# The last two steps of a graph network: products three blocks behind the sums, 62 row buffers, bias and residual from PSUM

## The chip, the core and the metric

The kernel runs on one core of one Trainium2 chip. A core has TensorE (PE in the profile), VectorE (DVE), ScalarE (ACT), GpSimd (POOL) and SyncE (SP), which run side by side and wait for each other through semaphores, and 16 DMA engines that move data between the chip's memory (DRAM) and the on-chip memories SBUF and PSUM. SBUF has 128 partitions. PSUM, where TensorE writes, has eight banks of 128 x 512 float32. The metric is the device time of one launch in microseconds (us); lower is better.

## The reference

Two layers over a graph of N = 10000 nodes and E = 160000 edges, with rows of 512 float32 numbers. The first layer (a relational layer with layer norms and a small MLP) isn't touched here. The second is two SAGE steps:

```python
def _sage_layer(h, src, dst, W_self, W_neigh, b, n_nodes):
    agg = jax.ops.segment_sum(h[src], dst, num_segments=n_nodes)
    deg = jax.ops.segment_sum(jnp.ones_like(dst, dtype=h.dtype), dst, num_segments=n_nodes)
    h_neigh = agg / jnp.maximum(deg, 1.0)[:, None]
    return jax.nn.relu(h @ W_self + h_neigh @ W_neigh + b)

h = jnp.maximum(_layernorm(x, axis=-1), 0.0)
x = x + _L1_gnn_ref(h, src, dst, ...)     # two calls of _sage_layer, one after the other
```

Each step gathers one row of `h` per edge, sums the rows by target node, divides by the degree, multiplies node and mean by a 512 x 512 matrix each, and adds a bias. The second step's output is added to `x`.

## The kernel before, in words

Three parts run one after the other. The first makes the per-relation products of all nodes and, beside them, sorts the edges into lists: for each block of 128 nodes, twelve lists of one edge per node (`row1` for the SAGE steps) and a list of at most 720 more edges for the nodes with a higher degree (`ovr1`), as six tiles of up to 128 rows. The second part is the first layer's sums with its MLP. The third part, two SAGE steps from line 764 on, is what the change touches. There are 79 blocks: the last one has 16 nodes and is taken first.

One block of a SAGE step goes like this. `gather` (line 493) issues 18 indirect DMAs on POOL, six for the longer list and then twelve with one row per node, each into a buffer of a ring of 32 (`RING`). `hots` (L505, VectorE) makes a 0/1 matrix that sends the 720 rows to their nodes; `sums` (L516, TensorE) multiplies it with the six tiles and leaves the sum in a PSUM bank `pa`, of which there are two. `add` (L527, VectorE) adds the twelve other tiles to it in place. ScalarE scales it by 1/degree into `m` (L822). `transposed` (L159 on TensorE, L160 on ScalarE) turns `m` into `mT`, and likewise the block's own rows `hb`, loaded by `load` (L780), into `hT` (`turn`). Four matmuls with `wss` (L825) and four with `wns` (L795) go to one bank `po`. `finish` adds the bias (L798, VectorE) and then, in the first step, applies ReLU on ScalarE (L804) and stores to `h2_d` (L805), or, in the second, takes the maximum with 0 and adds the residual `res` (L800, loaded at L784), and stores to `out` (L802). Float32 matmuls show in the profile as two records each.

The order is written out by hand: each engine runs its instructions in the order in which the program names them, and waits on semaphores where a value isn't there. The tile framework sets these waits, also for a buffer that is to be used again. In iteration i of a step the order is: load block i+2; mask of i+1; adds of i; scaling of i; the products of i with `wss`; `finish` of i-1, which holds its products with `wns`; `turn` of i+1; gathers and sums of i+1; transposes of `m` of i. All loads and stores of a step go through SP's queue, all gathers through POOL's. A step can gather only when the step before has stored all its rows.

Of the kernel before, what the change touches and what calls it, by code (L numbers as in the profile page):

```python
# [21 lines left out]
def kernel(  # L22
# [455 lines left out]
    def aligned(ctxa):  # L478

        gat = ctxa.enter_context(tc.tile_pool(name="gat", bufs=1))  # L480
        psA = ctxa.enter_context(tc.tile_pool(name="psA", bufs=2, space=PSUM))
        RING = 32
# [3 lines left out]
        def height(b):  # L486
            return min(P, N - b * P)

        def gather(b, table, row, ovr):

            def rows(n, idx):
                t = gat.tile([P, D], F32, name="rows", bufs=RING)
                nc.gpsimd.indirect_dma_start(  # L493
                    out=t[:n], out_offset=None, in_=table,
                    in_offset=bass.IndirectOffsetOnAxis(ap=idx, axis=0))
                return t[:n]

            others = [rows(n, ovr[:n, b, t:t + 1]) for t, n in enumerate(ov_tiles(b))]
            r = height(b)
            return others, [rows(r, row[:r, b, t:t + 1]) for t in range(T)]  # L500
# [29 lines left out]
        with ExitStack() as s:  # L530
            wp = s.enter_context(tc.tile_pool(name="wp2", bufs=1))
# [231 lines left out]

        for step, (h_d, ws, wn, bs) in enumerate(((h1_d, ws1, wn1, bs1), (h2_d, ws2, wn2, bs2))):
            with ExitStack() as s:
                wp = s.enter_context(tc.tile_pool(name="wp3", bufs=1))
                ip = s.enter_context(tc.tile_pool(name="ip", bufs=2))
                psT = s.enter_context(tc.tile_pool(name="psT3", bufs=3, space=PSUM))
                psO = s.enter_context(tc.tile_pool(name="psO3", bufs=3, space=PSUM))
# [5 lines left out]
                loaded, hTs = {}, {}  # L775

                def load(b):
                    r = height(b)
                    h = ip.tile([P, D], F32, name="hb", bufs=4)
                    nc.sync.dma_start(h[:r], h_d[b * P:b * P + r, :])  # L780
                    res = None
                    if step:
                        res = ip.tile([P, D], F32, name="res", bufs=5)
                        nc.sync.dma_start(res[:r], xn_d[b * P:b * P + r, :])  # L784
                    loaded[b] = (h, res)

                def turn(b):
                    r = height(b)
                    hTs[b] = ip.tile([P, KC, P], F32, name="hTb")
                    transposed(psT, hTs[b][:, :, :r], loaded[b][0][:r], r)  # L790

                def finish(b, po, mT):
                    r = height(b)
                    for k in range(KC):
                        nc.tensor.matmul(po[:r], mT[:, k, :r], wns[:, k, :], start=False,  # L795
                                         stop=(k == KC - 1))
                    o = ip.tile([P, D], F32, name="ob", bufs=3)
                    nc.vector.tensor_tensor(o[:r], po[:r], bss[:r], op=OP.add)  # L798
                    if step:
                        nc.vector.scalar_tensor_tensor(o[:r], o[:r], 0.0, loaded[b][1][:r],  # L800
                                                       op0=OP.max, op1=OP.add)
                        nc.sync.dma_start(out[b * P:b * P + r, :], o[:r])  # L802
                    else:
                        nc.scalar.activation(o[:r], o[:r], AF.Relu)  # L804
                        nc.sync.dma_start(h2_d[b * P:b * P + r, :], o[:r])  # L805
                    del loaded[b]

                for b in blocks[:2]:
                    load(b)
                turn(blocks[0])  # L810
                before = None
                held = begin(blocks[0], hots(blocks[0]), h_d, row1, ovr1)
                for i, b in enumerate(blocks):
                    r = height(b)
                    if i + 2 < len(blocks):
                        load(blocks[i + 2])
                    if i + 1 < len(blocks):
                        hot = hots(blocks[i + 1])
                    pa, own = held
                    add(b, pa, own)  # L820
                    m = ip.tile([P, D], F32, name="mb")
                    nc.scalar.activation(m[:r], pa[:r], AF.Copy, scale=rdeg[:r, b:b + 1])  # L822
                    po = psO.tile([P, D], F32, name="po3")
                    for k in range(KC):
                        nc.tensor.matmul(po[:r], hTs[b][:, k, :r], wss[:, k, :], start=(k == 0),  # L825
                                         stop=False)
                    if before:
                        finish(*before)
                    if i + 1 < len(blocks):
                        turn(blocks[i + 1])  # L830
                        held = begin(blocks[i + 1], hot, h_d, row1, ovr1)
                    mT = ip.tile([P, KC, P], F32, name="mTb")
                    transposed(psT, mT[:, :, :r], m[:r], r)
                    before = (b, po, mT)
                finish(*before)
# [308 lines left out]
```

## Time and profile before

| | us |
|---|---|
| median of 3 runs | 7879.0 (7872.07 to 7888.42) |
| profiled execution | 7907.2 |
| its span, first to last instruction | 7905.4 |
| first gather of the first layer's sums, in the span | 1591.5 |
| first gather of the first SAGE step | 3786.7 |
| first gather of the second SAGE step | 5844.8 |

The profile is of one execution. PE, DVE, ACT and POOL stand for the engines; PEld are TensorE's weight loads. A row of the groups gives line, engine, operation, output and inputs, the number of instructions, then their busy time and the mean in ns, then the idle time of the engine ahead of them and what ended most of it ("remote" is another core or an unknown queue, "issue" is time in which the profile shows nothing that was waited for). In the order of time a line has its start, its length, the engine, and in brackets how long the engine stood idle before it. Matmuls' ends are modelled in this profile. Over the whole span PE was busy 70%, DVE 47%, POOL 53%, ACT 13%; the DMA engines moved 182 GB/s.

### The profile page before, as it was taken

How to read it: one execution, taken by the hardware profiler on the slowest of the kernel's cores; microseconds unless marked ns; L12 is line 12 of the kernel's file. 1: busy time of each engine (PE TensorE's matmuls, PEld its weight loads, DVE VectorE, ACT ScalarE, POOL GpSimd, SP SyncE). 2: the span in 40 equal slices, each digit the busy share in tenths (PEclk: the TensorE clock that was granted, in tenths of full speed). 3: DMA queues.
4: the chain of work that ended last, by engine and by line, in shares of the span. 5: the costliest groups of instructions: out<-in, count | busy, mean ns of one | idle time of the engine just before them, and what ended most of it. 6: DMA issues, size and time to landing. Idle time of an engine off the chain costs nothing.

```text
span 7905.4 us, 50392 instructions
## 1 busy us (share of the span) xinstructions
PE 5555.9 (70%) x13686; PEld 2485.8 (31%) x13686; DVE 3693.7 (47%) x6357; ACT 1016.7 (13%) x1667; POOL 4174.9 (53%) x4346
## 2 busy tenths in 40 slices
PE   6969999947888888888555555665555665555565
PEld 3434444413333333334222222222222222222222
DVE  5424666345666666665243333344334444334434
ACT  0000000012222222223100000000000000000000
POOL 0030000066666666663566666666656666666665
PEclk9989999968888888889777787777777777777777
DMA  3232222266777777774566666666656666676765
GB/s 141 96 103 96 101 101 93 82 194 199 221 217 211 216 213 216 215 217 143 176 201 198 197 204 201 201 200 198 198 173 210 210 210 207 208 215 211 211 211 173
DMA packets 492503, 1441.17 MB, mean 182 GB/s; under 512 B 85650, under 2 KB 85650, under 8 KB 482082
## 3 DMA queue, kind: packets, MB, share of 16 engines
q0 software_dynamic: 337136, 1088.57, 47.1%
q1 hardware_dynamic: 141170, 262.13, 9.5%
q10 hardware_dynamic: 13904, 87.17, 2.8%
q8 instruction: 111, 1.82, 0.1%
q14 instruction: 182, 1.49, 0.1%
HBM read 1230.52 MB, written 207.01 MB: 182 GB/s over the span
## 4 chain that ended last, share of the span: by engine, by line
PE 41%; issue 26%; another core or an unknown queue 22%; DVE 4%; ACT 3%; DMA 2%; POOL 2%; ACTq 0%; POOLq 0%; DVEq 0%
PE pm L459 17%; PE pa L516 7%; PE ph L598 6%; PE po L608 5%; PE po L795 3%; PE po L825 3%; DVE pa L527 2%; POOL rows L493 2%; ACT hTb L160 1%; PE pT L159 1%; DMA n_i<-in_dst_dram 0%; ACT mTb L160 0%; DMA rows<-h_d,ovr 0%; DMA rows<-hall_d,row 0%
## 5 line engine op out<-in xcount | busy, mean ns | idle before, releaser
L527 DVE TENSOR_TENSOR pa<-pa,rows 128x512 f32<-128x512 f32 (+1 forms) x2844 | 1987.0, 699 | 1575.3 <-issue 1134.2
L493 POOL DMA_INDIRECT rows<-h_d,row x1896 | 1822.3, 961 | 1004.1 <-issue 498.4
L795 PE MATMUL po<-wns,mTb 128*128 128x512 f32 (+1 forms) x1264 | 753.2, 751 | 1260.6 <-issue 722.3
L516 PE MATMUL pa<-rows,hot 128*128 128x512 f32 (+2 forms) x2814 | 1331.5, 618 | 181.6 <-issue 141.9
L493 POOL DMA_INDIRECT rows<-hall_d,row x948 | 938.0, 989 | 506.2 <-issue 224.5
L493 POOL DMA_INDIRECT rows<-h_d,ovr x938 | 889.7, 948 | 488.1 <-issue 213.1
L459 PE MATMUL pm<-wrel,hT 128*128 128x512 f32 (+1 forms) x2528 | 1100.2, 593 | 18.2 <-issue 18.2
L493 POOL DMA_INDIRECT rows<-hall_d,ovr x469 | 445.1, 949 | 1222.0 <-issue 1146.8
L825 PE MATMUL po<-wss,hTb 128*128 128x512 f32 (+1 forms) x1264 | 716.0, 719 | 424.4 <-ACT hTb L160 322.9
L795 PEld LDWEIGHTS po<-wns,mTb 128*128 128x128 f32 (+1 forms) x1264 | 298.7, 244 | 1700.8 <-issue 1132.7
L516 PEld LDWEIGHTS pa<-rows,hot 128*128 128x128 f32 (+2 forms) x2814 | 539.8, 197 | 853.5 <-issue 800.1
L598 PE MATMUL ph<-x1T,w1s 128*128 128x512 f32 (+2 forms) x1344 | 616.0, 612 | 205.8 <-issue 143.0
L798 DVE TENSOR_TENSOR ob<-po,bss 128x512 f32<-128x512 f32 (+1 forms) x158 | 108.7, 688 | 1288.3 <-remote 978.3
L459 PEld LDWEIGHTS pm<-wrel,hT 128*128 128x128 f32 (+1 forms) x2528 | 478.0, 189 | 627.4 <-issue 609.0
L608 PE MATMUL po<-w2s,hid 128*128 128x512 f32 (+1 forms) x1264 | 592.5, 615 | 84.6 <-issue 74.1
L825 PEld LDWEIGHTS po<-wss,hTb 128*128 128x128 f32 (+1 forms) x1264 | 278.4, 232 | 759.8 <-issue 420.6
L462 DVE TENSOR_TENSOR ha<-pm,brel 128x512 f32<-128x512 f32 (+1 forms) x316 | 217.8, 690 | 582.5 <-PE pm L459 539.0
L598 PEld LDWEIGHTS ph<-x1T,w1s 128*128 128x128 f32 x1344 | 267.1, 207 | 525.0 <-issue 444.3
L608 PEld LDWEIGHTS po<-w2s,hid 128*128 128x128 f32 (+1 forms) x1264 | 242.1, 195 | 393.4 <-issue 374.0
L459 PE MATMUL pm<-wself,hT 128*128 128x512 f32 (+1 forms) x632 | 296.3, 611 | 55.9 <-issue 33.7
L160 ACT COPY mTb<-pT 128x512 f32<-128x512 f32 (+1 forms) x158 | 92.1, 583 | 1716.2 <-remote 1472.6
L340 POOL IOTA tags<- 128x79 f32 x1 | 0.3, 282 | 446.3 <-DVE first_i L329 446.3
(174 smaller groups left out, 3297.7 us busy)
## 6 DMA issues: line engine op xcount, KB each, us to landing
hall_d<-ha ACTq DMA_DIRECT2D x78, 1024.0 KB
hb<-h_d SPq DMA_DIRECT2D x156, 256.0 KB
rows<-h_d,row POOLq DMA_INDIRECT x1896
xs<-xs_d SPq DMA_DIRECT2D x78, 256.0 KB
xr<-xr_d SPq DMA_DIRECT2D x78, 256.0 KB
xn_d<-xr SPq DMA_DIRECT2D x78, 256.0 KB
h_d<-h SPq DMA_DIRECT2D x78, 256.0 KB
h_d<-ob SPq DMA_DIRECT2D x78, 256.0 KB
```

Of the source, the lines that this page charges most:

```text
L159: nc.tensor.transpose(p[:, k, :r], rows[:, k * P:(k + 1) * P], ident[:r, :r])
L160: nc.scalar.copy(dest, p[:, :, :r])
L459: nc.tensor.matmul(pm[:r], hT[:, k, :r], w[:, k, :], start=(k == 0), stop=(k == KC - 1))
L462: nc.vector.tensor_tensor(ha[:r, j - 1, :], pm[:r], brel[:r, (j - 1) * D:j * D], op=OP.add)
L493: nc.gpsimd.indirect_dma_start(out=t[:n], out_offset=None, in_=table, in_offset=bass.IndirectOffsetOnAxis(ap=idx, axis=0))
L516: nc.tensor.matmul(pa[:r], hot[:k, t, :r], o, start=(t == 0), stop=(t == n - 1))
L527: nc.vector.tensor_tensor(pa[:r], pa[:r], t, op=OP.add)
L598: nc.tensor.matmul(ph[:, :n], w1s[:, k, f * P:(f + 1) * P], self.xT[:, k, :n], start=(k == 0), stop=(k == KC - 1))
L608: nc.tensor.matmul(po[:r], self.hid[:, f, c * r:(c + 1) * r], w2s[:, f, :], start=(f == 0), stop=(f == FC - 1))
L795: nc.tensor.matmul(po[:r], mT[:, k, :r], wns[:, k, :], start=False, stop=(k == KC - 1))
L798: nc.vector.tensor_tensor(o[:r], po[:r], bss[:r], op=OP.add)
L825: nc.tensor.matmul(po[:r], hTs[b][:, k, :r], wss[:, k, :], start=(k == 0), stop=False)
```

## The change

The two SAGE steps get their own ring of 62 row buffers and three banks for `pa` (the first layer keeps 32 and two); both are now opened in each step by `buffers`. The products with `wss` and `wns` move into one function, `products`, which runs three blocks behind the sums (`LAG = 3`); `hT`, `mT` of up to four blocks are kept. The order of iteration i becomes: load `hb` of i+2; load `res` of i-2; mask of i+1; products of i-3; `turn` of i; gathers and sums of i+1; adds and scaling of i; `finish` of i-3; transposes of `m` of i. Three more iterations close the step. `po` has two banks in place of three, `hb` three buffers in place of four, `res` three in place of five. In the second step the bias is added in place in PSUM, and the residual add reads that bank in place of `ob`.

```diff
@@ aligned
-        gat = ctxa.enter_context(tc.tile_pool(name="gat", bufs=1))
-        psA = ctxa.enter_context(tc.tile_pool(name="psA", bufs=2, space=PSUM))
-        RING = 32
+        gat, psA, ring = None, None, 0
...
+        def buffers(s, n, blocks):
+
+            nonlocal gat, psA, ring
+            gat = s.enter_context(tc.tile_pool(name="gat", bufs=1))
+            psA = s.enter_context(tc.tile_pool(name="psA", bufs=blocks, space=PSUM))
+            ring = n
+
...
-                t = gat.tile([P, D], F32, name="rows", bufs=RING)
+                t = gat.tile([P, D], F32, name="rows", bufs=ring)
...
         with ExitStack() as s:
+            buffers(s, 32, 2)
             wp = s.enter_context(tc.tile_pool(name="wp2", bufs=1))
...
+        LAG = 3
         for step, (h_d, ws, wn, bs) in enumerate(((h1_d, ws1, wn1, bs1), (h2_d, ws2, wn2, bs2))):
             with ExitStack() as s:
+                buffers(s, 62, 3)
                 wp = s.enter_context(tc.tile_pool(name="wp3", bufs=1))
-                ip = s.enter_context(tc.tile_pool(name="ip", bufs=2))
+                ip = s.enter_context(tc.tile_pool(name="ip", bufs=4))
                 psT = s.enter_context(tc.tile_pool(name="psT3", bufs=3, space=PSUM))
-                psO = s.enter_context(tc.tile_pool(name="psO3", bufs=3, space=PSUM))
+                psO = s.enter_context(tc.tile_pool(name="psO3", bufs=2, space=PSUM))
...
                 def load(b):
                     r = height(b)
-                    h = ip.tile([P, D], F32, name="hb", bufs=4)
...
+                    hbs[b] = ip.tile([P, D], F32, name="hb", bufs=3)
+                    nc.sync.dma_start(hbs[b][:r], h_d[b * P:b * P + r, :])
+
+                def load_res(b):
+                    r = height(b)
+                    ress[b] = ip.tile([P, D], F32, name="res", bufs=3)
+                    nc.sync.dma_start(ress[b][:r], xn_d[b * P:b * P + r, :])
...
-                def finish(b, po, mT):
+                    transposed(psT, hTs[b][:, :, :r], hbs.pop(b)[:r], r)
+
+                def products(b):
                     r = height(b)
-                    for k in range(KC):
-                        nc.tensor.matmul(po[:r], mT[:, k, :r], wns[:, k, :], start=False,
-                                         stop=(k == KC - 1))
+                    hT, mT = hTs.pop(b), mTs.pop(b)
+                    po = psO.tile([P, D], F32, name="po3")
+                    for t, w, first in ((hT, wss, True), (mT, wns, False)):
+                        for k in range(KC):
+                            nc.tensor.matmul(po[:r], t[:, k, :r], w[:, k, :],
+                                             start=(first and k == 0),
+                                             stop=(not first and k == KC - 1))
+                    return po
+
+                def finish(b, po):
+                    r = height(b)
                     o = ip.tile([P, D], F32, name="ob", bufs=3)
-                    nc.vector.tensor_tensor(o[:r], po[:r], bss[:r], op=OP.add)
                     if step:
-                        nc.vector.scalar_tensor_tensor(o[:r], o[:r], 0.0, loaded[b][1][:r],
+                        nc.vector.tensor_tensor(po[:r], po[:r], bss[:r], op=OP.add)
+                        nc.vector.scalar_tensor_tensor(o[:r], po[:r], 0.0, ress.pop(b)[:r],
                                                        op0=OP.max, op1=OP.add)
                         nc.sync.dma_start(out[b * P:b * P + r, :], o[:r])
                     else:
+                        nc.vector.tensor_tensor(o[:r], po[:r], bss[:r], op=OP.add)
                         nc.scalar.activation(o[:r], o[:r], AF.Relu)
                         nc.sync.dma_start(h2_d[b * P:b * P + r, :], o[:r])
...
+                n = len(blocks)
                 for b in blocks[:2]:
                     load(b)
-                turn(blocks[0])
-                before = None
                 held = begin(blocks[0], hots(blocks[0]), h_d, row1, ovr1)
-                for i, b in enumerate(blocks):
-                    r = height(b)
-                    if i + 2 < len(blocks):
+                for i in range(n + LAG):
+                    b = blocks[i] if i < n else None
+                    old = blocks[i - LAG] if i >= LAG else None
+                    if i + 2 < n:
                         load(blocks[i + 2])
-                    if i + 1 < len(blocks):
+                    if step and 0 <= i - LAG + 1 < n:
+                        load_res(blocks[i - LAG + 1])
+                    if i + 1 < n:
                         hot = hots(blocks[i + 1])
-                    pa, own = held
-                    add(b, pa, own)
-                    m = ip.tile([P, D], F32, name="mb")
-                    nc.scalar.activation(m[:r], pa[:r], AF.Copy, scale=rdeg[:r, b:b + 1])
-                    po = psO.tile([P, D], F32, name="po3")
-                    for k in range(KC):
-                        nc.tensor.matmul(po[:r], hTs[b][:, k, :r], wss[:, k, :], start=(k == 0),
-                                         stop=False)
-                    if before:
-                        finish(*before)
-                    if i + 1 < len(blocks):
-                        turn(blocks[i + 1])
+                    if old is not None:
+                        po = products(old)
+                    if b is not None:
+                        turn(b)
+                        pa, own = held
+                    if i + 1 < n:
                         held = begin(blocks[i + 1], hot, h_d, row1, ovr1)
-                    mT = ip.tile([P, KC, P], F32, name="mTb")
-                    transposed(psT, mT[:, :, :r], m[:r], r)
-                    before = (b, po, mT)
-                finish(*before)
+                    if b is not None:
+                        r = height(b)
+                        add(b, pa, own)
+                        m = ip.tile([P, D], F32, name="mb", bufs=3)
+                        nc.scalar.activation(m[:r], pa[:r], AF.Copy, scale=rdeg[:r, b:b + 1])
+                    if old is not None:
+                        finish(old, po)
+                    if b is not None:
+                        mTs[b] = ip.tile([P, KC, P], F32, name="mTb")
+                        transposed(psT, mTs[b][:, :, :r], m[:r], r)
```

## The prediction

> **What bounds it now.** I read four views. First, the busy time by stretch, for the two stretches that the change touches: the two SAGE steps, which begin with POOL's first gather at 3786.7 and 5844.8 us and end at 5844.8 and 7905.4.
>
> ```profile
> core 0: us, PE busy (x) PEld busy (x) DVE busy (x) ACT busy (x) POOL busy (x), PEclk, DMA share, GB/s
> 3787.00:5845.00 2058.00, 1192.32 (x2834) 533.34 (x2834) 780.85 (x1106) 184.49 (x316) 1350.53 (x1418) 0.77 0.66 197
> 5845.00:7905.00 2060.00, 1202.44 (x2834) 537.18 (x2834) 832.58 (x1183) 134.93 (x237) 1361.20 (x1417) 0.77 0.69 207
> ```
>
> No engine is full. With 79 blocks (the first has 16 rows) a step is 26.05 us per block. Second, the groups of the first step.
>
> ```profile
> L493 POOL DMA_INDIRECT rows<-h_d,row x948 | 903.2, 953 | 490.2 <-issue 240.8 <-remote 161.1 <-PE pa L516 50.6
> L527 DVE TENSOR_TENSOR pa<-pa,rows 128x512 f32<-128x512 f32 (+1 forms) x948 | 662.4, 699 | 758.1 <-issue 727.4 <-ACT hTb L160 0.5
> L798 DVE TENSOR_TENSOR ob<-po,bss 128x512 f32<-128x512 f32 (+1 forms) x79 | 54.5, 690 | 520.1 <-remote 327.6 <-PE pa L516 124.9 <-PE pT L159 28.3
> ```
>
> DVE accounts for the whole step: 780.9 busy + 758.1 idle ahead of the adds + 520.1 idle ahead of the bias add = 2059. So per block DVE works 9.9 us and waits 9.6 + 6.6 = 16.2. POOL, third view (its waits), pauses far less:
>
> ```profile
> POOL rows L493 <- issue: 347.8, 1141, 0.3
> POOL rows L493 <- remote: 215.3, 122, 9.7
> POOL rows L493 <- PE pa L516: 50.9, 16, 6.1
> ```
>
> "issue" is the fixed 0.30 us between two gathers; the other two, some 266 us, are waits for a row buffer to come free. Gather to gather is 1.25 us (0.95 + 0.30) when nothing waits. Fourth, the order in time, here in mid-step.
>
> ```profile
> 4964.51 0.69 DVE L798 TENSOR_TENSOR ob<-po,bss 128x512 f32<-128x512 f32 x1 [0.23 <-PE po L795]
> 4964.75 5.32 PE L516 MATMUL pa<-rows,hot 128*128 128x512 f32 x12
> 4965.12 0.95 DVE L505 TENSOR_TENSOR hot<-lane,loc 128x768 f32<-128x768 f32 x1
> 4969.90 0.60 PE L159 MATMUL pT<-ident,mb 128*128 128x128 f32 x4
> 4970.34 3.60 PE L825 MATMUL po<-wss,hTb 128*128 128x512 f32 x8
> ...
> 4981.02 0.95 POOL L493 DMA_INDIRECT rows<-h_d,row  x1 [0.36 <-remote]
> 4984.54 0.95 POOL L493 DMA_INDIRECT rows<-h_d,ovr  x1 [2.58 <-remote]
> 4985.77 4.37 DVE L527 TENSOR_TENSOR pa<-pa,rows 128x512 f32<-128x512 f32 x6 [19.71 <-issue]
> 4987.21 0.59 ACT L160 COPY mTb<-pT 128x512 f32<-128x512 f32 x1 [18.49 <-remote]
> ```
>
> The adds at 4985.77 need the sums recorded at 4964.75 to 4970.07, and their own rows, whose last gather was issued at 4958.2. They start 15.7 us after the sums' record ends; ACT's copy of mTb starts 16.7 us after the transposes it needs. Consumers learn of PE's work late while POOL gathers. Once the gathers end it is otherwise:
>
> ```profile
> 5817.33 5.32 PE L516 MATMUL pa<-rows,hot 128*128 128x512 f32 x12
> 5822.74 8.77 DVE L527 TENSOR_TENSOR pa<-pa,rows 128x512 f32<-128x512 f32 x12 [4.27 <-issue]
> ```
>
> There the adds start 0.1 us after the sums. So the loop PE to DVE (and ACT) to PE sets the pace, stretched by late news from PE, and POOL's pauses follow from it: rows aren't consumed, so the ring of 32 (1.8 blocks of 18) fills.
>
> **What the Trainium skill says.** Perfetto Trace Analysis, section Tensor Engine Instruction: a matmul's end in the profile is estimated from its size, and its semaphore update comes later, with PSUM's acknowledgement. The trace agrees and is stronger: up to 16 us lie between. TensorE: Matmul & The Clock Gate, HAM oscillation: PE gaps over some 3.4 us put the clock to half. Here 0.77 is granted in both steps. GPSIMD Engine Reference, Specifications: POOL shares its SBUF interface with VectorE, and instructions with two SBUF inputs contend. Weakly seen: a gather beside the mask of L505 took 1.46 at 5018.51, and row gathers average 970 ns in the last step, where L800 reads two SBUF operands, against 953 in the one before.
>
> **The change, part by part** (sums against the profiled execution, span 7905.4, its time 7907.2; the median of the runs, 7879.0, is 28 below, so I take 28 off at the end).
>
> *Work.* None is removed or added: per block still 6 + 8 matmuls, 8 transposes, 12 adds, mask, bias add, ReLU or residual, 18 gathers, one or two loads and a store. Bias in place in PSUM costs as L527 does (699 against 690 ns): 79 x 0.009 = 0.7 us. The residual from PSUM: 0 to 16 us gained on POOL (948 x 17 ns), taken as 0, since other causes could make the 17 ns.
>
> *62 row buffers.* 3.4 blocks in place of 1.8. Alone it removes nothing: the average rate is that of consumption. Its worth is that POOL need not stop when DVE is one wait late. POOL's queue holds gathers alone, in the order of before. That the ring and the sums' banks are opened anew in each step costs 0: the first gather waits for the last store of the step before anyway. At most it gives POOL's waits back: gaps between a step's gathers above 1.6 us add up to 246 us in the first step and 249 in the second. Floor of a step's gathers: 1417 x 1.254 = 1777 us.
>
> *The order.* Before, in iteration i, DVE's bias add of i-1 waits for four matmuls L795 that themselves wait for mTb(i-1), and the adds of i+1 wait for sums that stand on PE behind those and behind turn(i+1). Two waits a block, each on fresh PE work. After, PE holds: products(i-3), turn(i), sums(i+1), transposes of m(i). The inputs of the first three are ready before add(i) begins, so PE goes through them without asking DVE or ACT; only the last stops for m(i). In recorded time: 7.2 + 0.6 + 5.3 + 0.6 = 13.7 us a block, 17.8 at a clock of 0.77. DVE spends 8.77 in add(i) meanwhile. The bias add of i-3 comes after add(i): products need 7.2 to 9.4, so its wait of 6.6 goes to about 0 (bounds 0 and 6.6). The wait ahead of the adds shrinks but stays: DVE needs 10.4 us a block (11.1 with residual), PE 13.7 to 17.8, and news is late. The six sums are mostly what is outstanding, in place of four transposes and six sums; I take 6 us, bounds 0 and 12. DVE's loop becomes 10.4 + 0 to 12 = 10.4 to 22.4, against POOL's 18 x 1.254 = 22.57. So the next bound is POOL. Behind a waiting DVE add stand only the bias add of i-3 and the next mask; behind PE's wait for m(i), products(i-2), not urgent. Third bank of pa: sums(i+1) needs only m(i-2) done, no wait; two banks of po suffice, as finish(i-5) is long over.
>
> *SP.* hb goes two blocks ahead with three buffers (the third waits for turn(i-1)), res one block ahead of its use, then the store. A load lands in some 3 to 5 us and has 22; cost 0, and 22 per block only if a load missed a whole period.
>
> *DMA.* 0.66 x 26.05/23 = 0.75 share. Gathers land about 3.3 us after their issue at full rate, so no backlog; cost 0.
>
> *The end of each step.* Products of three blocks now come after the last transposes: two more than before of 7.2 (13 at half clock), with bias and store. Before, from last gather to the next step or the end were 37 and 40 us. I add 18 (bounds 10 and 30) each.
>
> *Sum.* A step: 1777 + 38 + 18 = 1833, and 20 us (0.25 a block) of rest pauses: 1853, twice 3706. Before: 7905.4 - 3786.7 = 4118.7. Gain 413. 7905.4 - 413 - 28 = about 7465. Without pauses and with 10 at the ends 7408; with 5% of pauses (89 a step) and 30 at the ends 7627.
>
> **Rivals.** *Partly paid (17%).* DVE keeps about 13 to 14 us of waiting, as each wait hangs on late news whatever the order. For it: 4 outstanding matmuls cost 11 us before 4954.05 and 10 instructions 20 us before 4985.77, so the price is per item. Against it: much has already run when DVE arrives. At 24.5 a block a step is 16 + 78 x 24.5 + 56 = 1983; total about 7725.
>
> *The lag doesn't matter, only gathers do (3%).* The pauses stay, since consumption stays: 7879 plus 36 for the ends at most. Against it: DVE, not POOL, is idle for longest.
>
> *Slower (20%).* POOL's pauses are what lets PE's news through: at 4954 and 4985 DVE wakes while POOL stands. With 62 buffers POOL pauses less, and news gets later. At the start of the step, with POOL running freely, the adds of the second block waited 34.3 us, the longest of the step. It decides when DVE's wait passes 25.8 - 10.4 = 15.4 us a block; with 17, a block is 27.4: 158 x 1.6 + 36 = 290 more, 8170. Against it: DVE was busy adding at 4955 to 4964 with POOL at full rate, and PE's news was on time.
>
> **How the numbers follow.** POOL as the bound 60% (7405 to 7630), partly paid 17%, no effect 3%, slower 20%. 0.2% is about what a measurement of this kernel can tell. Faster 0.77, same 0.03, slower 0.20. The range leaves the slower case out: 7405 to 7880. Likeliest 7465, its own range 7405 to 7630.
>
> **What would show it.** Right: the two steps shrink from 2058 and 2060 to about 1850 each; POOL's gathers run at 1.25 us with pauses under 40 us a step; the idle time ahead of the bias add (520 us) nearly vanishes; DMA share near 0.75. Wrong: POOL still pauses by over 150 us a step, the idle time ahead of the adds grows past 1000 us, or the end of a step lasts over 80 us after its last gather.

## The result and the profile after

The changed kernel takes 7954.6 us (median of 4 runs, 7947.7 to 7962.8) against 7883.7 for the kernel before on the same chip (4 runs, 7872.1 to 7894.5): ratio 1.0091, interval 1.0071 to 1.0110. It is slower by about 71 us. The forecast was 7465. In the sessions of the experiments one and the same kernel, the one before, took either about 7890 us, as here, or about 7125; each run below is set beside the kernel before in its own session.

First the busy time by stretch of the changed kernel's profiled execution (span 7960.5): the gathers of the first step, from first to last issue, the end of that step, and the same for the second.

```profile
core 0: us, PE busy (x) PEld busy (x) DVE busy (x) ACT busy (x) POOL busy (x), PEclk, DMA share, GB/s
3806.60:5813.90 2007.30, 1119.16 (x2676) 497.60 (x2677) 750.46 (x1062) 168.87 (x298) 1349.68 (x1417) 0.76 0.68 200
5813.90:5882.10 68.20, 61.35 (x160) 28.02 (x158) 31.91 (x47) 11.03 (x19) 0.95 (x2) 0.96 0.15 48
5882.10:7887.50 2005.40, 1094.51 (x2685) 493.92 (x2686) 798.07 (x1131) 131.27 (x225) 1356.58 (x1417) 0.75 0.70 210
7887.50:7960.50 73.00, 59.02 (x149) 26.81 (x148) 36.34 (x52) 7.24 (x12) 0.93 (x1) 0.90 0.18 58
```

Set beside the trace of before, this gives the whole difference of the two spans:

| us | before | after | |
|---|---|---|---|
| up to the first layer's first gather | 1591.5 | 1592.5 | +1.0 |
| first layer (its code is unchanged) | 2195.2 | 2214.1 | +18.9 |
| step 1, first to last gather | 2021.1 | 2007.3 | -13.8 |
| step 1, after its last gather | 37.0 | 68.2 | +31.2 |
| step 2, first to last gather | 2020.4 | 2005.4 | -15.0 |
| step 2, after its last gather | 40.2 | 73.0 | +32.8 |
| span | 7905.4 | 7960.5 | +55.1 |

The remaining 16 us to 71 lie in which execution was profiled: before's (7907.2) is 23 above its median, after's 8. So the 14 and 15 us by which the gathers shrank, from one execution of each kernel, may be that difference and not the change's doing. The gathers were to shrink to about 1800 us a step; the ends grew by 1.7 and 1.8 times what was forecast. GpSimd's gaps between gathers still add up to 239 and 238 us a step (246 and 249 before; gaps of over 1.6 us, each counted above the usual 1.25). The groups of the first step and GpSimd's waits in it:

```profile
L498 POOL DMA_INDIRECT rows<-h_d,row x948 | 909.5, 959 | 515.0 <-remote 230.0 <-issue 221.1 <-DMA rows<-h_d,row 22.8
L532 DVE TENSOR_TENSOR pa<-pa,rows 128x512 f32<-128x512 f32 (+1 forms) x948 | 662.4, 699 | 655.7 <-issue 557.1 <-remote 37.4 <-DMA rows<-h_d,row 12.5
L821 DVE TENSOR_TENSOR ob<-po,bss 128x512 f32<-128x512 f32 (+1 forms) x79 | 54.6, 691 | 634.4 <-remote 574.1 <-issue 41.5 <-PE po L807 18.9
```

```profile
POOL rows L498 <- issue: 349.6, 1140, 2.6
POOL rows L498 <- remote: 230.0, 60, 19.6
```

VectorE's wait ahead of the bias add (L821, 520.1 us before) has grown to 634.4; the wait ahead of the adds (L532, 758.1 before) has shrunk to 655.7. Their sum was 1278 and is 1290. The order of time shows why, in a stretch of two blocks (51.2 us here) that recurs, with some exceptions in the first step, through both:

```profile
4994.18 5.32 PE L521 MATMUL pa<-rows,hot 128*128 128x512 f32 x12
...
4999.77 3.60 PE L807 MATMUL po<-wss,hTb 128*128 128x512 f32 x8
5003.21 3.60 PE L807 MATMUL po<-wns,mTb 128*128 128x512 f32 x8
5006.64 0.60 PE L159 MATMUL pT<-ident,hb 128*128 128x128 f32 x4
...
5014.40 8.77 DVE L532 TENSOR_TENSOR pa<-pa,rows 128x512 f32<-128x512 f32 x12 [18.79 <-issue]
...
5029.54 0.94 POOL L498 DMA_INDIRECT rows<-h_d,row  x1 [0.30 <-issue]
5034.23 0.69 DVE L821 TENSOR_TENSOR ob<-po,bss 128x512 f32<-128x512 f32 x1 [11.07 <-remote]
5034.31 0.58 ACT L160 COPY hTb<-pT 128x512 f32<-128x512 f32 x1 [15.85 <-remote]
5034.59 0.94 POOL L498 DMA_INDIRECT rows<-h_d,row  x1 [4.10 <-remote]
```

The adds at 5014.40 need the sums recorded from 4994.18 to 4999.50: 14.9 us late. The bias add at 5034.23 and the copy at 5034.31 need products and transposes recorded by 5006.8 and 5007.2: 27 us late, though by the record TensorE's work was over 16 and 11 us before VectorE and ScalarE came to wait for it (at 5023.2 and 5018.5). They start when GpSimd has stood still since 5030.5 (its last gather's record ends there). A count is one step of a semaphore, by which an engine tells the others that an instruction is done; from 5033.98 on, fifteen counts of TensorE's semaphore are recorded within 0.56 us. As the ends of matmuls are modelled, the record doesn't tell whether the work itself ended late or only the word of it; "late results" below means either.

This recurs. GpSimd stops for over 3 us 78 times in the two steps, most often 36 gathers after the last stop. In 73 of them a burst of TensorE's counts comes, in the median 5.3 us (first step) and 5.5 us (second) after the end of the last gather's record, or 2.9 and 3.1 us after its last transfer; GpSimd gathers again some 0.45 us later. Not every count waits for a stop: of the 955 recorded during the first step's gathers 430 come more than 3 us after the end of a gather's record, the others sooner, most of them while gathers follow each other.

### The profile page after: what moved, and what is told of

It reads as the page before. It is cut to its first block, busy times and chain, and to the rows that moved or that the text cites. A ratio compares the mean times of both kernels' runs of the same rounds, so it can differ in the third digit from the quotient of the medians.

```text
span 7960.5 us, 49894 instructions
## 1 busy us (share of the span) xinstructions
PE 5484.5 (69%) x13686; PEld 2460.8 (31%) x13686; DVE 3696.5 (46%) x6357; ACT 1014.3 (13%) x1667; POOL 4173.2 (52%) x4346
## 4 chain that ended last, share of the span: by engine, by line
PE 48%; another core or an unknown queue 31%; issue 11%; ACT 3%; POOL 3%; DVE 2%; DMA 2%; ACTq 0%; POOLq 0%; DVEq 0%
PE pm L459 17%; PE po L807 11%; PE pa L521 8%; PE po L614 5%; PE ph L604 4%; POOL rows L498 3%; PE pT L159 2%; DVE pa L532 1%; ACT mb L849 1%; ACT mTb L160 1%; DMA n_i<-in_dst_dram 0%; DMA rows<-hall_d,row 0%; DMA rows<-hall_d,ovr 0%; ACT hT L160 0%
## 5 line engine op out<-in xcount | busy, mean ns | idle before, releaser
L532 DVE TENSOR_TENSOR pa<-pa,rows 128x512 f32<-128x512 f32 (+1 forms) x2844 | 1986.9, 699 | 1467.7 <-issue 946.6
L521 PE MATMUL pa<-rows,hot 128*128 128x512 f32 (+2 forms) x2814 | 1437.9, 644 | 657.1 <-issue 508.5
L159 PE MATMUL pT<-ident,mb 128*128 128x128 f32 (+1 forms) x632 | 133.8, 349 | 1299.4 <-ACT mb L849 1232.9
L807 PE MATMUL po<-wss,hTb 128*128 128x512 f32 (+1 forms) x1264 | 697.3, 703 | 0.0
L807 PE MATMUL po<-wns,mTb 128*128 128x512 f32 (+1 forms) x1264 | 568.2, 592 | 0.0
L159 PEld LDWEIGHTS pT<-ident,mb 128*128 128x128 f32 (+1 forms) x632 | 94.8, 177 | 1524.6 <-ACT mb L849 1412.8
L816 DVE TENSOR_TENSOR po<-po,bss 128x512 f32<-128x512 f32 (+1 forms) x79 | 55.2, 698 | 770.5 <-remote 746.1
L160 ACT COPY hTb<-pT 128x512 f32<-128x512 f32 (+1 forms) x158 | 91.8, 581 | 2045.2 <-remote 1333.8
L821 DVE TENSOR_TENSOR ob<-po,bss 128x512 f32<-128x512 f32 (+1 forms) x79 | 54.6, 691 | 634.4 <-remote 574.1
```

What stands on the lines that cost most here:

```text
L159: nc.tensor.transpose(p[:, k, :r], rows[:, k * P:(k + 1) * P], ident[:r, :r])
L160: nc.scalar.copy(dest, p[:, :, :r])
L521: nc.tensor.matmul(pa[:r], hot[:k, t, :r], o, start=(t == 0), stop=(t == n - 1))
L532: nc.vector.tensor_tensor(pa[:r], pa[:r], t, op=OP.add)
L807: nc.tensor.matmul(po[:r], t[:, k, :r], w[:, k, :], start=(first and k == 0), stop=(not first and k == KC - 1))
L816: nc.vector.tensor_tensor(po[:r], po[:r], bss[:r], op=OP.add)
```

## The experiments

The theories. **B**: order and ring set the waits, as the prediction had it. **A**, first form: the number of TensorE's counts a block sets the pace. **A'**: TensorE's results come late while GpSimd gathers, whatever the order. **D**: TensorE's own work sets it. **E**, **F**, **G**, **K** are told where they are tested. The sessions in which the kernel before took about 7890 us are called late sessions below, those at about 7125 prompt ones; the expectations call them the slow and the fast kind of chip. **H** is that only late sessions have late results.

**Ring and order, each alone.** e1 is the kernel before with the larger ring:

```diff
-        RING = 32
+                buffers(s, 62, 2)      # in each SAGE step; first layer 32, 2
```

> The order of before, with only the ring of row buffers raised from 32 to 62 in the last two steps (two banks of sums, residual and bias as in before). Theory A (the pace is set by how TensorE's counts get out while GpSimd gathers, about 22 counts per block; the ring only decides when GpSimd stops): the pauses come in the same total, about 240 us a step, the first six blocks of each step run at 22.5 us and one long pause follows; 7879 within 0.3 %. Theory B (the reordering is what costs the 71 us, the ring alone would have paid): GpSimd's pauses fall to under 100 us a step and the time to about 7600. Theory C (a deeper ring makes TensorE's news later, my slower rival): 8000 or more.

e2 is the changed kernel with the smaller ring:

```diff
-                buffers(s, 62, 3)
+                buffers(s, 32, 3)
```

> The changed kernel with its ring put back from 62 to 32 in the last two steps; the order three blocks behind, the third bank of sums and the adds from PSUM stay. Theory A: period per block 25.5 to 25.8 us as in both kernels, ends of the steps 68 to 73 us after the last gather as in the changed kernel; within 0.3 % of the changed kernel, so about 7950 (0.9 % over before). Theory B (ring and order pay only together or the ring hurts): under 7890 if the ring was what hurt, over 8050 if the ring was paying for the order.

Measured: e1 7916.4 against 7893.8, ratio 1.0031 (1.0019 to 1.0044); e2 7909.1, ratio 1.0020 (1.0002 to 1.0039). By stretch (columns as above), the first step of e1, then of e2:

```profile
3786.20:5793.70 2007.50, 1134.29 (x2724) 508.85 (x2725) 751.20 (x1064) 173.64 (x302) 1349.63 (x1416) 0.76 0.67 201
5793.70:5842.20 48.50, 40.61 (x112) 18.62 (x110) 30.12 (x44) 8.42 (x15) 1.35 (x1) 1.00 0.17 55
```

```profile
3791.60:5797.10 2005.50, 1147.05 (x2750) 509.70 (x2750) 760.39 (x1075) 172.67 (x304) 1355.25 (x1417) 0.76 0.67 201
5797.10:5849.50 52.40, 37.83 (x85) 16.56 (x84) 21.11 (x31) 7.04 (x12) 0.90 (x1) 0.89 0.14 46
```

The gathers take 2005 to 2009 us in both steps of both, with pauses of 240 and 242 us in e1, 235 and 239 in e2. In before, after, e1 and e2 the long pauses lie mostly 36 gathers, two blocks, apart, with a ring of 32 as with one of 62. So B falls: neither part pays, and neither pays with the other. C falls too: e1 is far below its 8000. e2 is also below what its expectation held (about 7950): its ends are 52.4 and 44.2 us, not 68 to 73.

**Fewer counts, same matmuls.** The builder adds to TensorE's semaphore after each matmul in these steps because they stand under a run-time choice between two ways of summing; without the choice it folds a group's counts into its last matmul. The general way, which these data don't take, is left out of e3 (from the changed kernel) and e4 (from before):

```diff
-    with tc.If(go > 0) as cmp:
-        with ExitStack() as ctxa:
-            with tc.manual_schedule():
-                aligned(ctxa)
-    with cmp.Else():
-        general()
+    with ExitStack() as ctxa:
+        with tc.manual_schedule():
+            aligned(ctxa)
```

> The changed kernel with the run-time choice between the two ways of summing left out (the data here take the first way anyway; the other way is left out of the program). The builder then folds the counts of a group of matmuls into its last one: the 8 products count once, the 4 transposes of a block count once each time, so about 9 counts per block in place of 22, from the same matmuls in the same order. Theory A: the counts that must get out per block fall by more than half, GpSimd's pauses nearly vanish, the period falls from 25.5 to 22.5-23.3 us per block, a step to 1860-1910 us and the kernel to 7450-7650. Theory D (the matmuls themselves, their throttled clock or the transfers set the pace, counts do not matter): period stays at 25.5, 7930 to 7960.

> The kernel before, with the same edit: the run-time choice and the other way left out, counts folded to about 9 per block, ring of 32, order unchanged. Theory A: the period falls from 25.75 to 22.5-23.5 us and the kernel to 7450-7650, with the shorter ends of before (37 to 40 us), so about 60 us below the changed kernel with the same edit, unless the ring of 32 is now what stops GpSimd; then the changed kernel is the faster of the two. Theory D: 7850 to 7890.

Measured: e3 7933.7, ratio 1.0055 (1.0037 to 1.0072); e4 7877.1, ratio 0.9979 (0.9969 to 0.9989). Pauses 233 and 237 us a step in e3, 231 and 238 in e4. The first form of A falls, and both expectations missed by 230 us or more: the counts are late, but not because there are many. Leaving out the choice is worth some 0.2 % (e4 against before) to 0.35 % (e3 against after); e4 is the only complete kernel here that is below the kernel before, and it serves only data that fit. The busy time around one stop in e3's second step shows how late they can be:

```profile
6835.00:6843.60 8.60, 0.15 (x1) 0.00 (x0) 0.00 (x0) 0.00 (x0) 6.47 (x7) 0.50 0.71 204
6843.60:6845.50 1.90, 0.00 (x0) 0.00 (x0) 0.00 (x0) 0.00 (x0) 0.00 (x0) 0.50 0.66 190
6845.50:6848.85 3.35, 0.00 (x0) 0.00 (x0) 0.00 (x0) 0.00 (x0) 0.00 (x0) 0.50 0.00 0
6848.85:6852.00 3.15, 1.80 (x6) 1.28 (x7) 3.02 (x5) 1.76 (x3) 2.44 (x2) 0.50 0.30 61
```

GpSimd's last gather ends at 6843.3, the last transfer ends at 6845.5, and for 3.35 us no engine and no transfer is recorded as busy. At 6848.89 eight counts come within 0.31 us, and VectorE, ScalarE and GpSimd start at 6848.91, 6848.97 and 6849.25. The last matmul ahead of these counts is recorded from 6834.14 to 6835.15; the products that VectorE's bias add needs are recorded by 6821.54, 27 us before it starts.

**No gathers.** e5, and the same kernel again as e10, fetch the same bytes into the same tiles by plain transfers from SyncE's queue; e14 and e18 issue those transfers from GpSimd. The rows are 128 consecutive ones, not those of the graph's edges.

```diff
+                if ring == 62:
+                    asked = (asked + 97) % full
+                    nc.sync.dma_start(t[:n], table[asked * P:asked * P + n, :])
+                    return t[:n]          # e14, e18: nc.gpsimd.dma_start
                 nc.gpsimd.indirect_dma_start(
```

> The changed kernel, with the row tiles of the last two steps fetched as plain transfers of 128 consecutive rows from SyncE's queue in place of gathers by GpSimd (same bytes into the same tiles, other rows, so the sums are of the wrong rows; GpSimd is idle). Theory A' (TensorE's counts come late because of GpSimd's gathers, not because of the bytes): counts come on time, the waits of 11 and 20 us per two blocks on VectorE go, a block takes 13 to 18 us by VectorE or TensorE and a step under 1450 us. Theory F (the transfers' traffic delays the counts or is itself the bound at about 185 GB/s): a block stays at 25 us or longer. Theory D (TensorE's own work sets the pace): a block stays at about 25.5 us.

> The changed kernel with the rows of the last two steps fetched as plain transfers of 128 consecutive rows from SyncE's queue, GpSimd idle there (other rows, so the sums are wrong). It took 5833 on the fast kind of chip, 14 us a block. Theory A' on the slow kind: the first three quarters of the time (first layer, still with gathers) as slow as ever, the two steps as on the fast chip, 14 to 15 us a block, counts on time: 6450 to 6550. If the late counts are a matter of that chip's TensorE or of traffic and not of the gathers: a block stays at 20 us or more, 7000 or more.

> The changed kernel with the rows of the last two steps fetched by GpSimd as plain transfers of 128 consecutive rows (other rows, so the sums are wrong), drawn again. On the fast kind of chip it took 5827, as from SyncE's queue. On the slow kind: if any dense stream of transfers that GpSimd issues holds TensorE's results back, a block takes over 18 us, GpSimd pauses, and the kernel is over 6600; if only the gathers do, the steps are as from SyncE's queue, 1163 us each, and the kernel at 6100 to 6250.

Measured: e5 5832.8, where the kernel before took 7122.2; e10 6144.0, where it took 7902.0; e14 5827.1 beside 7132.6; e18 6139.1 beside 7889.4. In e10 the first layer, still with gathers, is as slow as ever: its gathers take 2101 us, against 1824 in e5. The SAGE steps take 1137 and 1185 us in e10 and 1138 and 1186 in e5, 1117 and 1202 in e18 and 1118 and 1201 in e14. Without gathers the two kinds of sessions are alike. (e10's steps take the 14 to 15 us a block that were expected; its total lies 300 us below the expectation, whose sum was too high.) Of e10, then of e18, in order of time:

```profile
4503.56 0.60 PE L159 MATMUL pT<-ident,hb 128*128 128x128 f32 x4
4504.19 0.58 ACT L160 COPY hTb<-pT 128x512 f32<-128x512 f32 x1 [6.72 <-PE pT L159]
4504.81 5.53 PE L527 MATMUL pa<-rows,hot 128*128 128x512 f32 x12 [0.66 <-DMA rows<-h_d]
4510.44 8.77 DVE L538 TENSOR_TENSOR pa<-pa,rows 128x512 f32<-128x512 f32 x12 [3.71 <-PE pa L527]
```

```profile
4499.47 2.74 PE L527 MATMUL pa<-rows,hot 128*128 128x512 f32 x6
4502.31 8.87 DVE L538 TENSOR_TENSOR pa<-pa,rows 128x512 f32<-128x512 f32 x12 [3.61 <-PE pa L527]
...
4509.36 0.60 PE L159 MATMUL pT<-ident,hb 128*128 128x128 f32 x4
4510.00 0.58 ACT L160 COPY hTb<-pT 128x512 f32<-128x512 f32 x1 [6.72 <-PE pT L159]
```

Copy and adds start 0.03 and 0.10 us after the work they need in e10, 0.04 and 0.10 in e18, with 356 GB/s moving in e10's first step (195 in the changed kernel). So neither the amount of traffic (F) nor this order makes results late; nor, by e18, GpSimd's issuing of transfers as such. D falls too: TensorE does the same matmuls in 14.4 us a block. What is left is the gathers. Each of these four is a single run, but they lie 1290 to 1760 us below the kernel before. Whether it is the gathers' lists of rows or the scattered rows themselves wasn't separated.

**TensorE's and VectorE's work, ScalarE's order.** e6 does sums and adds on 128 of 512 columns and fills the rest of `m` with copies. e8, and again e11, issue the copy of hTb behind `mb` on ScalarE.

```diff
+                w = P if ring == 62 else D          # e6; hot and rows as before
+                nc.tensor.matmul(pa[:r, :w], hot[:k, t, :r], o[:, :w], ...)
+                nc.vector.tensor_tensor(pa[:r, :w], pa[:r, :w], t[:, :w], op=OP.add)
```

```diff
                         nc.scalar.activation(m[:r], pa[:r], AF.Copy, scale=rdeg[:r, b:b + 1])
+                        keep(b, p)     # e8, e11: the copy to hTb, no longer in turn(b)
```

> The changed kernel with sums and adds of the last two steps on 128 of the 512 columns (the rest is filled with copies, so the output is wrong): TensorE's work of a block falls by some 4 us and VectorE's adds from 8.8 to about 3 us; gathers, counts and the order of all queues stay. Theory A': the period stays within 0.5 us of 25.5 us, since neither engine's work sets it. Theory D: it falls by 3 us or more, to GpSimd's 22.5.

> The changed kernel with one move on ScalarE's queue in the last two steps: the copy of the turned hb is issued behind the mb of the same block and no longer ahead of it, so mb, and with it the turning of m on TensorE, no longer waits for the count of the turning of hb. Theory E (the late count costs because TensorE waits for mb, mb stands behind the copy, and the copy waits for TensorE's count): GpSimd's long pauses shrink from 240 to under 120 us a step, period 23 to 24 us, kernel 7600 to 7750. Theory A' alone (any wait for TensorE's counts will do the same): within 0.5 % of the changed kernel.

> The changed kernel with the copy of the turned hb issued behind the mb of its block on ScalarE's queue. It was 0.5 % over before on the fast kind of chip, where there were no late counts to test. On the slow kind, theory E (one late count stops TensorE because mb stands behind that copy): GpSimd's long pauses shrink to under 120 us a step, 7600 to 7750. Theory A' alone: within 0.5 % of the changed kernel, 7900 to 7970.

Measured: e6 7140.2 and e8 7154.2 (ratio 1.0048, 1.0031 to 1.0065), both where the kernel before took 7122.2; e11 7944.5, ratio 1.0055 (1.0036 to 1.0074) to 7902.0. e6 therefore says nothing on late sessions. e8 shows a prompt one; the groups of its first step:

```profile
L532 DVE TENSOR_TENSOR pa<-pa,rows 128x512 f32<-128x512 f32 (+1 forms) x948 | 662.8, 699 | 1014.8 <-PE pa L521 631.8 <-DMA rows<-h_d,row 358.0 <-PE pT L159 16.3
L829 DVE TENSOR_TENSOR ob<-po,bss 128x512 f32<-128x512 f32 (+1 forms) x79 | 53.7, 680 | 23.2 <-PE po L815 12.4 <-issue 10.9
```

There GpSimd runs on (its gathers take 1785 and 1791 us a step, with pauses of 19 and 9), hardly a wait is left ahead of the bias add (23 us a step), and VectorE waits for rows and the sums of rows just landed. In e11 theory E fails: pauses 234 and 233 us. Yet the waits moved: 386 us ahead of the adds and 902 ahead of the bias add. Their sum is 1288.

**The lag.** e12 sets `LAG = 1` in the changed kernel; e9 is the changed kernel once more.

> The changed kernel itself, unaltered, once more beside the kernel before. Chips differ: on one the kernel before takes about 7890, on another about 7120 us. Theory H (on the slow kind TensorE's counts come late while GpSimd gathers, on the fast kind they do not): on the slow kind 0.7 to 1.1 % over before, with GpSimd's pauses of some 235 us a step; on the fast kind no pauses, 22.5 to 22.8 us per block, and 0.3 to 0.6 % over before, the longer ends alone. The prediction's reading (the waits are a matter of order and ring, on any chip): no such difference between chips.

> The changed kernel with the products one block behind the sums in place of three (62 buffers, three banks, adds from PSUM stay). If the lag is what lengthens the ends of the steps, each end is 14 to 20 us shorter than the changed kernel's (two blocks' products of 6.8 us and their finishing), and the kernel 28 to 40 us faster than it, on either kind of chip; the pauses on the slow kind stay. If the lag did take waits from VectorE: slower than the changed kernel by over 100 us on the slow kind.

Measured, in a late session: e9 7971.8, ratio 1.0087 (1.0062 to 1.0112) to 7902.0, pauses 234 and 237 us a step, as H has it (the changed kernel itself had no prompt session; e8 stands in for it); e12 7934.9, ratio 1.0040 (1.0019 to 1.0062). The first step of e12:

```profile
3785.00:5791.30 2006.30, 1143.70 (x2707) 516.34 (x2708) 750.45 (x1063) 170.51 (x300) 1343.97 (x1417) 0.76 0.68 201
5791.30:5844.10 52.80, 46.10 (x128) 21.38 (x126) 30.65 (x45) 9.96 (x17) 0.89 (x1) 1.00 0.15 50
```

The ends are 52.9 and 54.0 us, against 68.2 and 73.0 at a lag of three (66.7 and 72.8 in e9), and the kernel is 37 us faster than e9; the gathers take the same (2006 and 2009 us, 2007 in both steps of e9). The lag is paid at each end and buys nothing.

**TensorE kept busy; a thinner stream.** e10 leaves a doubt: there TensorE is busy nine tenths of the time, and perhaps it is an idle TensorE that holds results back (G). e7, e13 and e17 add transposes behind the sums, on e3:

```diff
+                p = filler.tile([P, KC, P], F32, name="pT")
+                for _ in range(24):
+                    nc.tensor.transpose(p[:, 0, :], ident, ident)
```

> The changed kernel with folded counts, and 24 extra transposes of a constant square behind the sums of each block of the last two steps (their result is not used), so that TensorE does not fall idle there. Theory G (counts of the last matmuls stay inside TensorE while it stands idle or at half clock, and are pushed out by matmuls that follow): the period falls from 25.5 to under 24 us. Theory A': no change but for the work itself, 25.5 to 27 us. Theory D: 28 us or more.

> The changed kernel with folded counts and 24 extra transposes of a constant square behind the sums of each block of the last two steps, drawn again for a chip of the slow kind. The rows from SyncE's queue made counts prompt there, but TensorE was then busy nine tenths of the time, so that run doesn't tell theory G (counts stay inside a TensorE that stands idle) from theory A' (the gathers hold them back). G: pauses gone, under 24 us per block, kernel 7500 to 7650. A': period 25.5 us or a little longer, pauses of 230 us or more a step, 7900 to 8000. On the fast kind: 7150 to 7170, as twice before.

e7 and e13 fell on prompt sessions (7152.8 and 7161.9 beside 7122.2 and 7132.6) and tell nothing of G. e17: 8087.9 against 7891.1, ratio 1.0250 (1.0233 to 1.0267), pauses 283 and 333 us a step, a block at 26.1 and 26.7 us where G had under 24. So G falls in this form, with TensorE busy 71% of the first step's gathers (56% in the changed kernel); the time is even above the 7900 to 8000 that A' had, so more TensorE work made it worse. In e17's second step some matmuls' starts are 2.1 to 2.8 us apart, with nothing waited for that the profile shows (0.43 us a record elsewhere: eight in 3.60). Between the first and last gathers of the first step TensorE stands idle for over 1 us without a recorded reason 101 times in the changed kernel, 115 times in e3 and 315 times in e17, and not once in e7, e8 and e13 (prompt) or e10 (no gathers). So where results are late TensorE itself is held up at times; why stays open. Of e17:

```profile
6999.97 1.01 PE L813 MATMUL po<-wns,mTb 128*128 128x512 f32 x1 [1.80 <-issue]
7002.76 1.01 PE L813 MATMUL po<-wns,mTb 128*128 128x512 f32 x1 [1.78 <-issue]
7004.86 1.01 PE L813 MATMUL po<-wns,mTb 128*128 128x512 f32 x1 [1.09 <-issue]
7007.65 1.01 PE L813 MATMUL po<-wns,mTb 128*128 128x512 f32 x1 [1.79 <-issue]
```

e15 and e16 put one and three fills of a 128x1 tile behind each gather of the kernel before:

```diff
+                for _ in range(1):              # e16: range(3)
+                    nc.gpsimd.memset(tick, 0.0)
```

> The kernel before (ring of 32, products one block behind), with one fill of a 128x1 tile on GpSimd behind each gather of all three passes. If the fill costs c, GpSimd's pace is 22.5 + 18c us per block. Theory K (the counts get through in GpSimd's own gaps, so a thinner stream of gathers replaces the pauses): the long pauses shrink by more than the fills cost, and the kernel is faster than before on the slow kind of chip if c is under 0.15 us. Theory A' (only a stop of GpSimd of some 3 us lets them through): pauses stay near 240 us a step and the time rises by up to 4251c. On the fast kind: slower by 3000 to 4251 times c.

> The same with three fills behind each gather, so three times the thinning: GpSimd's pace 22.5 + 54c us per block. Theory K: the long pauses are gone and the period is GpSimd's pace alone. Theory A': pauses of some 5.6 us per two blocks on top of that pace, so 25.5 + 54c us per block.

They took 7214.8 (ratio 1.0119, 1.0102 to 1.0136) and 10282.0 beside 7132.6, in a prompt session, and so leave K open. e16 shows that three fills stretch the gathers of a step to 2837 us and more. e15's ends are of use: with before's order and ring they last 16.8 and 19.7 us where nothing is late; e8's, at a lag of three and a ring of 62, 34.4 and 34.9.

## Why the prediction was wrong

**What bounds it.** The view was right: VectorE accounts for the step by work and two waits, and results are late while GpSimd gathers (15.7 and 16.7 us), not after. The conclusion drawn from it, "the loop PE to DVE (and ACT) to PE sets the pace", was the mistake: the runs show a rate that no arrangement of that loop moved. VectorE's two waits of the first step together, in us (its own work is the same in all of these, so a constant sum says that the step's length is):

| before | e1 | e2 | e3 | e4 | e11 | e12 | after |
|---|---|---|---|---|---|---|---|
| 1278 | 1272 | 1277 | 1288 | 1262 | 1288 | 1275 | 1290 |

**The order: the step that failed.** "PE goes through them without asking DVE or ACT": by the record it did, and it was of no use, since its results reached VectorE and ScalarE 15 to 27 us later all the same. It took for granted that work placed earlier on TensorE reaches the others earlier. The bias add's wait, taken as about 0 with 6.6 us a block as the upper bound, became 634.4 / 79 = 8.0 us; the adds' wait, taken as 6, became 8.3. Together 16.3 a block, where 16.2 had been; the sum had 6. The prediction knew that results come late; it allowed 6 us for that at the adds and nothing at the bias add, whose work would be long done. That is most of the missing gain: the gathers were to fall from 2021 to about 1797 us (1777 and 20 of pauses), and fell to 2007, 210 us a step, so 420 of the 490 us between forecast and result.

**62 buffers.** "Alone it removes nothing" holds (e1). What was added, that the ring gives GpSimd's waits back once VectorE is quicker, was never put to the test, as VectorE wasn't. Its cost at the ends was left out. With 62 buffers 36 adds, three blocks, start after the step's last gather is issued (e1, e12, after); in before it is 24 and 20.

**POOL as the next bound.** Right where nothing is late: in prompt sessions variants of the changed kernel run their gathers at 22.5 to 22.8 us a block (e6, e7, e8, e13). But there the kernel before already takes 7122 to 7133 us, so little is left for the change to win, and e8, the changed kernel but for one move on ScalarE, is 0.48 % slower, about what its longer ends cost. No trace of before showed such a session.

**The ends.** Forecast +18 each (10 to 30), measured +31.2 and +32.8, above the bounds. At a ring of 62 the lag's share (after against e12) is 15 and 19, as forecast; at a ring of 32 (e2 against before) it is 15 and 4. The ring's share was missing from the sum: 11.5 and 11.1 with before's order (e1 against before), 16 and 29 beside the lag of three (after against e2). The parts don't add up evenly, and each figure is of one execution. In prompt sessions lag and ring together cost 18 and 15 (e8 against e15).

**Nothing for SP, DMA, bank and residual** stands: no view of the changed kernel has them on the path. The 17 ns by which row gathers were longer in the second step were rightly not counted on: with the residual read from PSUM they still average 966 ns there and 959 in the first step (970 and 953 before).

**Rivals.** The one given 3 %, pauses stay and the ends cost 36, is what happened: 7879 + 36 = 7915 by it, 7954.6 measured. Between the two spans the steps give 35 of the difference. The first layer's 19 is open: its instructions are the same, and e1, e2, e11 and e12, with the same first layer, spent 2193, 2200, 2207 and 2193 us there, the changed kernel 2214 and again 2217 in e9. The partly paid one said that each wait hangs on late results whatever the order, and that was the mechanism; but VectorE's waits came to 16.3 us a block, not 13 to 14, and the price per item that spoke for it is not borne out, as 9 counts a block (by the program) in place of 22 changed little (e3, e4). The slower rival had seen that results get through when GpSimd stops, which the bursts bear out; but a deeper ring didn't lengthen VectorE's wait (16.3 a block, not 17). Of the signs named ahead the pauses spoke against the forecast (239 us against a bound of 150); the other two, over 1000 us ahead of the adds and ends of over 80 us, did not occur.

## What to carry to other kernels

When a consumer starts long after its producer's record ends, and only while a third engine streams, do not price a new order or a deeper ring at anything before a run without that stream has shown whether it is what holds the results back. If two waits trade places and their sum stays, the new order has not touched what sets the pace. A lag between stages of a loop that isn't bound by their order costs its length at every place where the loop must drain, here two times 15 to 19 us at a ring of 62.

## What the runs showed of the hardware

Two kinds of sessions, with one and the same kernel: 7884 to 7902 us (medians) and 7122 to 7133. The difference lies almost wholly in the three passes with gathers, the untouched first layer among them (its gathers 2063 to 2102 us against 1823 to 1826); up to the first gather they differ by some 12 us (1592 and 1580), and steps without gathers by 1. VectorE's add takes 699 ns in both (after, e8). The record has both kinds under the same chip number (2: e5 to e8 prompt, e18 late); if that number stands for one chip, the kind isn't a fixed property of it. What else sets it, no run here settles.

In late sessions TensorE's results come late while GpSimd's gathers stream: 15 to 27 us by the consumers' starts, and many at once, up to fifteen recorded some 40 ns apart (14 gaps in 0.56 us), when GpSimd has stopped, mostly 3.5 to 5.7 us after the end of its last gather's record. The Trainium skill, TensorE: Matmul & The Clock Gate, section The cost: per-tile semaphore tail, has such increments follow each other at 26.3 ns; the spacing here is longer, but of that order. So folding gains little: even fifteen counts in 0.56 us becoming eight in 0.31 at each of some 78 stops would save about 20 us, by this estimate; e4 gained 17. The spacing is not the delay. The cause of the delay inside the chip stays open. It goes with the gathers (e10, e18). It is not the number of counts (e3, e4), not the amount of traffic (e10), not transfers issued by GpSimd as such (e18), and 24 more matmuls a block don't lift it (e17). A thinner stream of gathers wasn't seen under it.
